# Four small layers on one core: factor sums shared with POOL, the last batch in query halves, due times by kind

## The chip, the cores and the metric

One core of one Trainium2 chip runs the whole program; the time is device microseconds of one execution, with everything read from and written to the chip's main memory inside it. A core has engines that run side by side, each with its own queue in a fixed order: PE (TensorE: matmuls, and transposes, which are matmuls with an identity), DVE (VectorE), ACT (ScalarE) and POOL (GpSimd). SP (SyncE) only issues transfers here; POOL issues some too. They wait for each other through semaphores. The times are medians of a few executions; the profile is of one further execution of the same kernel.

## The reference

All inputs are float32. The input x has 8 batches of 512 tokens by 512 features, and four layers follow, each with a layer norm before and another before its residual add:

```
x = x + LN(attn0(LN(x)))     # scores = x^T x over the token axis, softmax, context
x = x + LN(ffn0(LN(x)))      # sum over r of x @ factors[r], r = 0..7, / sqrt(8) + bias
x = x + LN(attn1(LN(x)))     # RMS norm, 8 query heads of 64, 2 key/value heads, Wo, skip
x = x + LN(ffn1(LN(x)))      # silu(x Wg * gs) * (x Wu * us), then Wd * ds; inner width 1408
```

Since the eight factor matrices meet the same x, their sum is made once, and one product with it serves. Gate, up and down weights are -1, 0 or 1.

## The kernel before

**Tiles.** A token tile is 128 tokens, so a batch has four (NT = 4), and the 512 features make four k tiles (KT = 4). The inner width of the last layer makes eleven inner tiles (NI = 11), kept in two tensors, hd0 with inner tiles 0 to 5 and hd1 with 6 to 10. Only one of each exists. The other tags used below: x (11 tiles), z and hl (2 each), e and wgu (4 each), and in PSUM five banks f and three banks g. Most matmuls are in full float32. The last layer's x and hd are split into a leading and a remaining part of a cheaper format, since its weights are exact in that format.

**Order.** Nothing is written down in the order in which it runs. Each stage records operations with an engine, an estimated duration, what they read and write, and a due time (`rec.prio`), counted in batches. `Recorder.issue` (L108) then plays the whole program with those estimates, and at each step, on each engine, takes among the operations that could start within `slack` of the first one that with the least due time; a buffer is taken when its first user starts and comes free after its last. The order so found is the order of each engine's queue on the chip, where it doesn't change any more. On PE an operation has a `state`, the shape in which it uses the array: 128x128, 64x128 (scores and transposes of attention 1, two row groups at once) or 128x64 (its weighted values, two column groups). A change of state costs 0.1 us in that reckoning. Stages of neighbouring batches overlap: while the second attention of batch b runs, the last layer of batch b-1 fills PE.

**The start.** `load_fixed` (L388) reads eight factor matrices in four k tiles each. For each k tile the first factor goes straight to `fsum` and the other seven to places of hd0 and hd1, from which DVE adds them in turn (L401), 28 adds in all. `look_at_low_bits` (L420) reads all gate, up and down weights once more into hd0 and hd1 and ORs them on DVE (33 operations, L442), into a z tile, to learn whether the cheaper format is exact; a second version of the program runs only if it is not. Weight loads of the last layer are issued by POOL (L372), the others by SP (L351).

**The stages.** `stage_attn0` makes scores row by row (L626, with transposes for the lower part, L624), a softmax (L551 maximum, L558 exponential, L568, L575), its transpose, and the context (L655). `stage_ffn0` takes a norm (L495 statistics, L500, L504 and L511 on POOL for the inverse deviation, L519 the normalize), transposes the tile (L587), multiplies by `fsum` (L677) and adds (L690). `add_layernorm` norms the result and adds it to x on POOL (L537). `stage_attn1` makes keys, values and queries (L809, L820, L838), for each of four head pairs and each query tile the scores (L869), softmax, transposes (L900), copies (L912), and for each two query tiles the weighted values (L931); then it projects the four token tiles (L959, L974). Its loops run over head pairs outside and halves of the query tiles inside. `stage_ffn1` norms and transposes the four token tiles, splits them (L990, L999), multiplies by gate and up (L1032, over 512 tokens), makes hd (L1052, L1062, L1071), splits it again, multiplies by down (L1100), scales (L1113), norms, adds and stores (L1123).

Of the kernel before, what the change touches and what calls it, by code (L numbers as in the profile page):

```python
# [12 lines left out]
I32 = mybir.dt.int32  # L13
# [40 lines left out]
class Recorder:  # L54
# [53 lines left out]
    def issue(self, places, slack=0.1):  # L108
# [26 lines left out]
        while left:  # L135
            best = None
            for e, ops in ready.items():
                able = [(s, op.prio, op.n, op) for op in ops if (s := start(op)) is not None]
                if not able:
                    continue  # L140
                first = min(able)[0]
                pick = min((p, n, s, op) for s, p, n, op in able if s <= first + slack)
                if best is None or (pick[2], pick[1]) < best[:2]:
                    best = (pick[2], pick[1], pick[3])
# [93 lines left out]
def layers(  # L238
# [99 lines left out]


# [48 lines left out]
    def load_fixed():  # L388
        rec.prio = 0.15

        slots = staging()
        for kt in range(KT):
            rec.prio = 0.15 + 0.01 * kt
            load(fsum, factors[0, ts(kt, P), :], part=kt, view=lambda t, kt=kt: t[:, kt, :])
            for r in range(1, R):
                f, j = next(slots)
                load(f, factors[r, ts(kt, P), :], part=j, view=lambda t, j=j: t[:, j, :])

                def go(f=f, j=j, kt=kt):
                    d = fsum.t[:, kt, :]  # L400
                    nc.vector.tensor_tensor(d, d, f.t[:, j, :], ALU.add)  # L401

                add("DVE", 0.69, go, reads=[(f, j)], writes=[(fsum, kt)])
        load(bias_bc, ffn_bias.partition_broadcast(P))
        rec.prio = 0.3
# [7 lines left out]
        rec.prio = 0.95  # L413
# [6 lines left out]
    def look_at_low_bits():  # L420

        low, most, total = Buf("z"), Buf("s1"), Buf("f")
        rec.prio = 1.0
        bits = lambda: low.t[:, :].bitcast(I32)
        add("DVE", 0.3, lambda: nc.vector.memset(bits(), 0), writes=[low])
        slots = staging()
        pieces = [(w, c) for w in (gate_t, up_t, down_t) for c in range(NI)]
        for n, (w, c) in enumerate(pieces):
            rec.prio = 1.0 + 0.01 * n
            raw, j = next(slots)  # L430
            if w is down_t:
                load(raw, w[ts(c, P), :], part=j, view=lambda t, j=j: t[:, j, :])
            else:
                load(
                    raw,
                    w[:, ts(c, P)].rearrange("(k p) n -> p k n", p=P),
                    part=j,
                    view=lambda t, j=j: blocks(t[:, j, :]),
                )

            def gather(raw=raw, j=j):
                nc.vector.tensor_tensor(  # L442
                    bits(), bits(), raw.t[:, j, :].bitcast(I32), ALU.bitwise_or
                )

            add("DVE", 0.69, gather, reads=[(raw, j)], writes=[low])
# [83 lines left out]
    def add_layernorm(xt, src, us=0.55):  # L530

        y = buf_of(src) if buf_of(src).tag == "z" else Buf("z")
        layernorm(whole(y), src, us)
        add(
            "POOL",
            1.27,
            lambda: nc.gpsimd.tensor_tensor(ap(xt), ap(xt), y.t[:, :], ALU.add),  # L537
# [69 lines left out]
    def stage_attn0(x, at, span):  # L607
        xn, xnT, wT = Buf("big"), Buf("big"), Buf("big")
        rec.prio = at
# [7 lines left out]
        for i in range(KT):  # L617
            rec.prio = at + span * (0.1 + 0.1 * i)
# [30 lines left out]
        for t in range(NT):  # L649
            rec.prio = at + span * (0.5 + 0.1 * t)  # L650
# [15 lines left out]
    def stage_ffn0(x, at, span):  # L666
        for t in range(NT):
            rec.prio = at + span * 0.2 * t
# [29 lines left out]
    def stage_attn1(x, at, span):  # L698
# [3 lines left out]
        for t in range(NT):  # L702
            rec.prio = at + span * 0.05 * t
# [97 lines left out]
        rec.prio = at + span * 0.2  # L801
# [28 lines left out]

        for i in range(NPAIR):
            rec.prio = at + span * (0.22 + 0.13 * i)
# [13 lines left out]
            asked = mm(pq, 3.43, queries, [wq, hT], room=[qT])  # L846
# [10 lines left out]
        wos = []  # L857
        for i in range(NPAIR):
            for u in range(2):
                aT = Buf("big")  # L860
                for s in (2 * u, 2 * u + 1):
                    rec.prio = at + span * (0.25 + 0.13 * i + 0.03 * s)
                    es = [Buf("e") for _ in range(G)]
                    scs = [Buf("f") for _ in range(G)]

                    def scores(i=i, s=s, scs=scs):
                        for g in range(G):
                            gp = ts(g, DH)
                            nc.tensor.matmul(  # L869
                                scs[g].t[:, :],  # L870
                                qT.t[gp, i, ts(s, P)],
                                kT.t[gp, :],
                                start=True,
                                stop=True,
                            )

                    add(
                        "PE",
                        0.87,
                        scores,  # L880
                        reads=[(qT, (i, u)), kT],
                        writes=scs,
                        room=[*es, aT],
                        state="64x128",
                    )
                    for g in range(G):
                        softmax_row(scs[g], es[g])


                    pts = [Buf("f") for _ in range(2)]  # L890

                    def halves(b):
                        return b.t[:, :].rearrange("p (c q) -> p c q", q=DH)

                    def transposes(es=es, pts=pts):
                        for g in range(G):
                            for t in range(NT):
                                for hf in range(2):
                                    hp = ts(hf, DH)
                                    nc.tensor.transpose(  # L900
                                        halves(pts[hf])[:, g * NT + t, :],
                                        es[g].t[hp, ts(t, P)],
                                        ident[hp, hp],
                                    )

                    add("PE", 0.56, transposes, reads=es, writes=pts, room=[aT], state="64x128")
                    for hf in range(2):

                        def place(hf=hf, s=s, aT=aT, pts=pts):
                            lo = s % 2 * P + hf * DH  # L910
                            copy = nc.scalar.copy
                            copy(columns_of(aT)[:, :, lo : lo + DH], halves(pts[hf]))  # L912

                        add(
                            "ACT",
                            0.6,
                            place,
                            reads=[pts[hf]],
                            writes=[(aT, 2 * s + hf)],
                        )  # L920
                rec.prio = at + span * (0.29 + 0.13 * i + 0.03 * s)
                po = Buf("f")

                def columns_of(b):
                    return flat(b.t).rearrange("p (c q) -> p c q", q=2 * P)

                def values_of(aT=aT, po=po):
                    for t in range(NT):
                        for g in range(G):
                            gp = ts(g, DH)  # L930
                            nc.tensor.matmul(  # L931
                                po.t[gp, : 2 * P],
                                v.t[:, t * P + g * DH : t * P + (g + 1) * DH],
                                columns_of(aT)[:, g * NT + t, :],
                                start=(t == 0),
                                stop=(t == NT - 1),
                            )

                attended = mm(po, 1.75, values_of, [aT, v], state="128x64")

                add(
                    "ACT",
                    0.4,
                    lambda i=i, u=u, po=po: nc.scalar.copy(
                        qT.t[:, i, ts(u, 2 * P)], po.t[:, : 2 * P]
                    ),
                    reads=[po],
                    writes=[(qT, (i, u))],
                )
            wos.append(Buf("ws"))  # L950
            load(wos[i], wo_t[ts(i, P), :], view=flat, after=[asked])

        for t in range(NT):
            rec.prio = at + span * (0.8 + 0.03 * t)
# [25 lines left out]
            add_layernorm(whole(x[t]), whole(z))  # L980
        return last
# [24 lines left out]
    def stage_ffn1(x, b, at, span, after):  # L1006
        PASS = 0.23 if split else 0.86
        xs = [Buf("hl") for _ in range(1 + split)]
        for t in range(NT):
            rec.prio = at + span * 0.01 * t  # L1010
            xn = Buf("row")
            mv, rstd = moments(whole(x[t]))
            normalize(whole(xn), whole(x[t]), mv, rstd, room=xs)
            pt = transpose_to(column(xs[0], t), whole(xn), copy=None, room=xs)
            in_parts([column(d, t) for d in xs], lambda pt=pt: blocks(pt.t), [pt], 0.6)

        hds = [Buf(f"hd{c}") for c in range(len(CUTS))]
        for c, (lo, hi) in enumerate(CUTS):
# [182 lines left out]
```

## Time and profile before

| what | value |
|---|---|
| median of 3 runs (lowest, highest) | 1568.37 us (1568.25, 1568.81) |
| the profiled execution | 1568.29 us |
| its span, first to last instruction | 1566.5 us |
| PE, DVE, ACT, POOL busy | 1503.5, 1080.4, 702.2, 566.4 us |
| mean clock of PE | 0.988 of full |
| moved by DMA | 105.87 MB, mean 68 GB/s |
| PE busy in 600:700 and in 700:800 | 100.00 and 98.10 us |

How to read the lines that follow. A line of the timeline gives start and length in microseconds, the engine, the line of the kernel, the operation, what it writes and reads, the shape, how many instructions are merged (x8), and in brackets how long the engine stood idle before it and what ended that. Matmuls overlap, so their lengths are a little longer than the distance from one to the next. A line of waits gives the total, how often and the longest. A full float32 product counts as two instructions. "Clock" is the share of PE's full clock that was granted.

### The profile page before, as it was taken

Reading aid. Unit: us, or ns where it says so; the run is one execution under the profiler, and the core shown is the slowest. Engines: PE = TensorE matmul, PEld = TensorE weight load, DVE = VectorE, ACT = ScalarE, POOL = GpSimd, SP = SyncE. Lnnn points to the kernel's source line nnn. Section 1 sums busy time; section 2 is a strip of 40 time slices with the busy share of each in tenths; the row PEclk is TensorE's granted clock in tenths of the full one; section 3 lists DMA queues with packets and bytes.
Section 4 is the critical chain, followed back from the end, with each engine's and each line's share of the span. In section 5 each row is a group of like instructions: output and inputs, shape, how many; then the busy total and the mean of one; then the engine's idle time right before and its main releaser. Section 6 shows DMA issues by size and latency. Waiting matters only on the chain.

```text
span 1566.5 us, 21966 instructions
## 1 busy us (share of the span) xinstructions
PE 1503.5 (96%) x7986; PEld 923.6 (59%) x7986; DVE 1080.4 (69%) x2226; ACT 702.2 (45%) x1448; POOL 566.4 (36%) x869
## 2 busy tenths in 40 slices
PE   6799999999999999999999999999999999999896
PEld 3354456665666646665566656666566665666485
DVE  6898865679557794587845788458865678557734
ACT  2045546541376324763257523575236742277221
POOL 3614341137410473115721257103651036411532
PEclk9899999999999999999999999999999999999999
DMA  9540043212331124302142132411233102330170
GB/s 346 165 155 1 1 101 75 44 52 54 74 75 28 41 57 91 62 28 72 30 89 53 40 75 42 88 35 48 61 61 81 21 34 61 74 75 14 35 132 31
DMA packets 152471, 105.87 MB, mean 68 GB/s; under 512 B 6945, under 2 KB 132897, under 8 KB 152353
## 3 DMA queue, kind: packets, MB, share of 16 engines
q0 software_dynamic: 94512, 49.03, 16.5%
q1 hardware_dynamic: 57840, 55.34, 11.3%
q8 instruction: 65, 1.06, 0.3%
q14 instruction: 54, 0.43, 0.1%
HBM read 95.96 MB, written 8.39 MB: 67 GB/s over the span
## 4 chain that ended last, share of the span: by engine, by line
PE 81%; DVE 9%; POOL 5%; DMA 2%; issue 2%; ACT 1%; SPq 0%; POOLq 0%; ACTq 0%; DVEq 0%
PE g L1032 21%; PE g L1100 11%; PE f L869 8%; PE f L931 7%; PE f L838 7%; PE f L677 7%; PE f L900 5%; PE f L959 4%; PE f L587 3%; PE f L626 3%; DVE row L519 3%; POOL rstd L511 2%; DVE st L495 2%; PE f L820 2%; PE f L809 2%
## 5 line engine op out<-in xcount | busy, mean ns | idle before, releaser
L1032 PE MATMUL g<-hl,wgu 128*128 128x512 f32 x1408 | 350.3, 400 | 0.7 <-ACT hl L990 0.7
L551 DVE TENSOR_REDUCE s<-f 128x1 f32<-128x512 f32 x288 | 186.5, 683 | 185.3 <-PE f L869 171.3
L1032 PEld LDWEIGHTS g<-hl,wgu 128*128 128x128 f32 x1408 | 258.9, 189 | 81.5 <-issue 18.4
L504 POOL TENSOR_SCALAR ve<-mv 128x1 f32<-128x1 f32 x224 | 71.1, 317 | 523.0 <-DVE mv L500 509.0
L558 ACT ACTIVATE e<-f,s 128x512 f32<-128x512 f32 x288 | 195.8, 688 | 87.0 <-DVE s L551 81.2
L537 POOL TENSOR_TENSOR x<-x,z 128x512 f32<-128x512 f32 x128 | 169.5, 1324 | 61.6 <-DVE z L519 53.1
L1100 PE MATMUL g<-wd,hl 128*128 128x512 f32 x704 | 180.7, 406 | 3.2 <-DVE hl L999 3.2
L912 ACT COPY big<-f 128x512 f32<-128x512 f32 x256 | 134.4, 597 | 60.1 <-PE f L900 59.2
L1100 PEld LDWEIGHTS g<-wd,hl 128*128 128x128 f32 x704 | 129.0, 189 | 45.0 <-issue 11.5
L372 POOL DMA_DIRECT2D wgu<-in_up_t x88 | 67.3, 765 | 235.9 <-PE g L1032 235.8
L575 DVE TENSOR_SCALAR e<-e,s 128x512 f32<-128x512 f32 x288 | 144.0, 500 | 10.2
L511 POOL TENSOR_TENSOR rstd<-ve,mhalf 128x1 f32<-128x1 f32 x224 | 143.1, 639 | 18.1
L869 PE MATMUL f<-kv,big 64*128 64x512 f32 x512 | 138.6, 628 | 0.0
L1062 DVE SCALAR_TENSOR_TENSOR sig<-g,gs,sig 128x512 f32<-128x512 f32 x88 | 65.8, 748 | 98.4 <-ACT sig L1052 98.4
L931 PE MATMUL f<-big,kv 128*64 128x256 f32 x1024 | 124.6, 385 | 0.0
L372 POOL DMA_DIRECT2D wgu<-in_gate_t x88 | 68.7, 781 | 140.3 <-PE g L1032 137.1
L677 PE MATMUL f<-fsum,rT 128*128 128x512 f32 x256 | 116.7, 604 | 0.7 <-ACT rT L591 0.7
L959 PE MATMUL f<-ws,big 128*128 128x512 f32 x256 | 114.9, 594 | 0.6 <-ACT big L794 0.6
L838 PE MATMUL f<-big,ws 128*128 128x512 f32 x256 | 114.1, 594 | 0.0
L655 PE MATMUL f<-big,big 128*128 128x512 f32 x256 | 112.3, 594 | 0.7 <-ACT big L591 0.7
L931 PEld LDWEIGHTS f<-big,kv 128*64 128x64 f32 x1024 | 67.8, 136 | 71.8 <-ACT big L912 13.8
L900 PEld LDWEIGHTS f<-ident,e 64*128 64x128 f32 x2048 | 71.7, 139 | 43.7 <-issue 32.0
(81 smaller groups left out, 1971.3 us busy)
## 6 DMA issues: line engine op xcount, KB each, us to landing
wgu<-in_gate_t POOLq DMA_DIRECT2D x88, 256.0 KB, 3.3
wgu<-in_up_t POOLq DMA_DIRECT2D x88, 256.0 KB, 3.4
x<-in_x SPq DMA_DIRECT2D x32, 256.0 KB, 2.7
ws<-in_wq_t SPq DMA_DIRECT2D x32, 256.0 KB, 3.3
ws<-in_wo_t SPq DMA_DIRECT2D x32, 256.0 KB, 2.6
out<-x SPq DMA_DIRECT2D x32, 256.0 KB, 2.0
hd<-in_factors SPq DMA_DIRECT2D x28, 256.0 KB, 5.4
wd<-in_down_t POOLq DMA_DIRECT2D x11, 256.0 KB, 8.1
```

Source lines behind the costliest of these rows:

```text
L511: lambda: nc.gpsimd.tensor_tensor(rstd.t[:, :], ve.t[:, :], mhalf, ALU.pow),
L537: lambda: nc.gpsimd.tensor_tensor(ap(xt), ap(xt), y.t[:, :], ALU.add),
L551: lambda: nc.vector.tensor_reduce(nmax.t[:, :], sc.t[:, :], AX.X, ALU.max, negate=True),
L558: lambda: nc.scalar.activation(e.t[:, :], sc.t[:, :], AF.Exp, bias=nmax.t[:, :], accum_out=tot.t[:, :]),
L677: nc.tensor.matmul(po.t[:, :], xnT.t[:, kt, :], fsum.t[:, kt, :], start=(kt == 0), stop=(kt == KT - 1),)
L838: nc.tensor.matmul(pq.t[:, :], wq.t[:, kt, :], hT.t[:, kt, :], start=(kt == 0), stop=(kt == KT - 1),)
L869: nc.tensor.matmul(scs[g].t[:, :], qT.t[gp, i, ts(s, P)], kT.t[gp, :], start=True, stop=True,)
L900: nc.tensor.transpose(halves(pts[hf])[:, g * NT + t, :], es[g].t[hp, ts(t, P)], ident[hp, hp],)
L931: nc.tensor.matmul(po.t[gp, : 2 * P], v.t[:, t * P + g * DH : t * P + (g + 1) * DH], columns_of(aT)[:, g * NT + t, :], start=(t == 0), sto ...
L959: nc.tensor.matmul(po.t[:, :], qT.t[:, i, ts(t, P)], flat(wos[i].t), start=(i == 0), stop=(i == NPAIR - 1),)
L1032: nc.tensor.matmul(bank.t[:, :], w.t[:, kt, :], d.t[:, kt, :], start=(n == 0), stop=(n == KT * len(xs) - 1),)
L1100: nc.tensor.matmul(po.t[:, :], ap(o)[:, it - lo, :], wd.t[:, it, :], start=(it == 0 and k == 0), stop=(it == NI - 1 and k == len(ops) - 1),)
```

## The change

- **Factor sums.** For k tiles 0 and 3 (`FSUM_POOL`) the seven adds each are made by POOL; tiles 1 and 2 stay on DVE.
- **Low bits.** The running OR moves from a z tile to a piece of hd, cleared by POOL, and gets later due times.
- **Last batch, second attention** (`EARLY`): the loops are turned, so that both query tiles of a half go through all head pairs and are projected before the second half begins. Wo is loaded with the first half.
- **Last batch, last layer:** norms by halves of the tokens, then the gate and up products of inner tiles 0 to 3 (`FEW`) for tokens 0 to 255 and, loaded again, for tokens 256 to 511; the other seven for all tokens. Down products are recorded after all of these.
- **Residual adds of the last batch** in attention 1 and the last layer go from POOL to DVE.
- **Order.** Due times come from a table, by kind of work and batch (`DUE`, `SHIFT`), slack is 0.1198, and on PE an operation in another state than the one held has 0.0066 added to its due time (`STAY`). Steps in the table count head pairs, halves, tiles. The gate step of the last batch is negative.

```diff
+                held = state.get(e)
+                pick = min(
+                    (p + (STAY.get(e, 0.0) if op.state not in (None, held) else 0.0), n, s, op)
+                    for s, p, n, op in able
+                    if s <= first + slack
+                )
...
+    def when(kind, b, *steps):
+        rec.prio = due(kind, b if b < B // 2 else b - B, B, *steps)
...
+                eng, us, on = (
+                    ("POOL", 1.27, nc.gpsimd) if kt in FSUM_POOL else ("DVE", 0.69, nc.vector)
+                )
...
-        low, most, total = Buf("z"), Buf("s1"), Buf("f")
+        most, total = Buf("s1"), Buf("f")
+        slots = staging()
+        low = next(slots)
+        add("POOL", 0.5, lambda: nc.gpsimd.memset(bits(), 0), writes=[low])
...
+        eng, took, on = ("DVE", 0.69, nc.vector) if last else ("POOL", 1.27, nc.gpsimd)
...
+        if split_up:
+            for u in range(2):
+                for i in range(NPAIR):
+                    attended = attend(i, u)
+                    if u == 0:
+                        load_wo(i)
+                for t in (2 * u, 2 * u + 1):
+                    when(kinds[2], b, t % 2, u)
+                    last = project(t, attended)
+                firsts.append(last)
...
+        if b in EARLY or b - B in EARLY:
+            rounds = [((0, 1), range(FEW)), ((2, 3), range(FEW)), (every, range(FEW, NI))]
+            kind = "h1."
...
+                    sig = Buf("sig" if len(toks) == NT else "e")
+                    pg, pu = Buf("g"), Buf("g" if len(toks) == NT else "f")
...
+                                        bank.t[:, cut],
+                                        w.t[:, kt, :],
+                                        d.t[:, kt, cut],
...
+                    after=products,
...
-AHEAD = 0.3
-ATTN0 = (0.0, 0.163)
-FFN0 = (0.476, 0.16)
-ATTN1 = (0.55, 0.6)
-FFN1 = (1.682, 0.337)
+DUE = {
+    "x": (0.0595,),
+    "fsum": (0.0844, 0.01),
+    "wd": (1.1173,),
+    "low": (1.3155, 0.01),
+    "a0.norm": (0.0803,),
+    "a0.row": (0.0175, 0.0195),
+    "a0.out": (0.2134, 0.0139),
+    "f0": (0.3719, 0.0331),
+    "a1.norm": (0.6166, 0.0452),
+    "a1.q": (0.6808, 0.1115),
+    "a1.row": (0.6967, 0.0723, 0.036, 0.0208),
+    "a1.mix": (0.7469, 0.0737, 0.036),
+    "a1.out": (1.0283, 0.0236),
+    "e1.row": (0.6591, 0.039, 0.1695, 0.0034),
+    "e1.mix": (0.9942, 0.0607, 0.1848),
+    "e1.out": (0.9884, 0.018, 0.141),
+    "f1.norm": (1.7342, 0.0089),
+    "f1.gate": (1.716, 0.0146),
+    "f1.down": (1.935, 0.019, 0.0131),
+    "h1.norm": (1.7316, -0.021, 0.095),
+    "h1.gate": (1.1851, -0.0129, 0.0932),
+    "h1.down": (1.935, 0.0236, 0.0091),
...
+SHIFT = {
+    ("a0", 0): -0.112,
+    ("a1", 0): 0.183,
+    ("f1", 0): -0.0585,
+    ("x", 1): 0.0585,
...
+STAY = {"PE": 0.0066}
+SLACK = 0.1198
+FSUM_POOL = (0, 3)
+EARLY = (-1,)
+FEW = 4
...
+def due(kind, b, n, *steps):
+    first, *more = DUE[kind]
+    at = first + (b if b >= 0 else b + n) + SHIFT.get((kind[:2], b), 0.0)
+    return at + sum(k * d for k, d in zip(steps, more))
```

## The prediction

> **What bounds the kernel now.** I read the page first, then PE's busy time by stretches, then the list of what PE waited for, then the timeline at the start, in a middle batch and at the end. The first fence is the page's busy line and two of PE's waits (total us, times, longest).
>
> ```profile
> PE 1503.5 (96%) x7986; PEld 923.6 (59%) x7986; DVE 1080.4 (69%) x2226; ACT 702.2 (45%) x1448; POOL 566.4 (36%) x869
> ...
> PE f L587 <- DVE row L519: 27.2, 12, 8.5
> PE f L624 <- ACT u L640: 3.7, 2, 3.1
> ```
>
> PE is the bound: 1503.5 of 1566.5 us, so all of its idle time is 63 us. Only two things can be won: that idle time, and work on PE that isn't arithmetic. The stretches tell where the idle time lies (columns: start and end, length, busy us of PE, PEld, DVE, ACT, POOL, then PE's clock).
>
> ```profile
> 0.00:57.26 57.26, 34.33 (x114) 19.93 (x115) 42.68 (x82) 10.96 (x22) 26.68 (x51) 0.91 0.95 308
> 57.26:61.50 4.24, 4.24 (x7) 1.86 (x7) 2.91 (x7) 0.59 (x1) 2.57 (x7) 0.57 0.22 62
> 1477.80:1488.80 11.00, 4.02 (x17) 2.58 (x17) 8.67 (x17) 2.39 (x5) 9.33 (x15) 0.64 0.32 59
> 1488.80:1493.00 4.20, 4.20 (x9) 3.08 (x10) 0.66 (x1) 1.33 (x2) 0.00 (x0) 0.50 0.51 94
> ```
>
> Before the first product with the factor sum, 57.26 us, PE idles for 23 us, and then runs four more at little over half clock. Ahead of the last batch's gate products PE does almost nothing for 11 us, and then starts cold. A stretch of 100 us in the middle shows PE at 98.1 to 100.0, and the waits there are one of 1.8 us per batch. After PE's last product at 1554.05 come 12.4 us of norm, add and store.
>
> **The start.** DVE holds it: 8.9 of every 10 us from 20 to 60. In its queue the 28 factor adds (20.1 us, 721 ns each in the group row) stand between the softmax rows and norms that PE waits for.
>
> ```profile
> 16.54 0.69 DVE L401 TENSOR_TENSOR fsum<-fsum,hd 128x512 f32<-128x512 f32 x1 [4.20 <-DMA hd<-in_factors]
> 23.09 0.33 PE L624 MATMUL f<-ident,u 128*128 128x128 f32 x1 [3.14 <-ACT u L640]
> 44.47 1.26 POOL L537 TENSOR_TENSOR x<-x,z 128x512 f32<-128x512 f32 x1 [0.93 <-DVE z L519]
> 45.12 1.88 DVE L401 TENSOR_TENSOR fsum<-fsum,hd 128x512 f32<-128x512 f32 x2
> 55.35 2.12 PE L587 MATMUL f<-ident,row 128*128 128x128 f32 x8 [8.46 <-DVE row L519]
> ```
>
> The first line shows DVE standing for a factor that hasn't landed, with batch 0's row maxima queued behind it; 3.14 of PE's wait follow from that. The last shows PE waiting 8.46 for the norm of the first tile of the factor layer, whose x was done at 41.84, but whose statistics stand in DVE's queue until 52.52, after the last add.
>
> What the change does here: k tiles 0 and 3 go to POOL, 14 adds. DVE loses 14 x 0.721 = 10.1 us, and the first landings, with 5.6 us of DVE waits in all, are waited for on POOL (0.00 busy from 20 to 30), where no norm of batch 0 stands behind them until 37. POOL gains 14 x 1.26 = 17.6 us by the L537 line above (1.65 where it was held up at 40.19). Tile 3's seven, about 9 us, fall where POOL also has the four norms and adds of the first layer, 2.05 each uncontended, so 17 us of POOL work from about 31 on. The eleven wd issues in POOL's queue are through by 13.2, before the first landing at 16.5, so the adds wait for none of them. What is queued behind a POOL add that waits for a late factor is the rstd of those norms; DVE's normalize waits for it, then PE. Batch 1's four x loads are due after the factors now, so the factor loads stand earlier in SP's queue: eight x loads take 4.72 us there before the first factor at 5.50, four of them about 2.4. The 33 loads and 33 ORs of the low bit check (757 ns each, 25 us of DVE, now in 52 to 136) move behind batch 1's first layers, and their running OR leaves the z tile for a piece of hd, so one of two z tiles comes free for the norms until 136 (counted at nothing: DVE sets the pace there). They hide under a DVE that is 57% busy from 200 to 300; without that cover they delay batch 0's gate products, since both use the hd tiles.
>
> Here a rule of the Trainium skill speaks against the change ("SBUF — State Buffer", Who interferes with whom): a DVE instruction with two SBUF inputs and a POOL instruction that reads SBUF exclude each other for the whole instruction. The trace agrees: the two adds at 45.12 take 1.88 and not 1.38, the extra 0.50 being about the rest of POOL's add from 44.47. By the group rows alone, DVE is relieved of 10.1 and up to 5.6 of waits: up to 15.7 earlier, limited by PE's contexts, which end at 46.9 and would end some 3 earlier. By the rule the adds hold the shared port 14 x 0.69 + 14 x 1.26 = 27.3 us in place of 19.3, so 8.0 of it come back: 2 to 8 earlier. Tile 0's adds fall where DVE has little that needs the port, so I charge the lock for tile 3's: 7 x (1.26 - 0.69) = 4.0. With half of the waits recovered, 10.1 + 2.0 - 4.0 makes 8. **Start: -8**, bounds -12 and 0.
>
> **The last batch.** Its second attention runs query tiles 0 and 1 through all four head pairs, projects them, then tiles 2 and 3. The gate and up products of inner tiles 0 to 3 are made once for each half of the tokens.
>
> ```profile
> 1467.22 10.57 PE L959 MATMUL f<-ws,big 128*128 128x512 f32 x24
> ...
> 1488.79 42.99 PE L1032 MATMUL g<-hl,wgu 128*128 128x512 f32 x176 [0.68 <-ACT hl L990]
> ...
> 1533.49 20.56 PE L1100 MATMUL g<-wd,hl 128*128 128x512 f32 x87 [1.36 <-DVE hl L999]
> ...
> 1557.34 1.26 POOL L537 TENSOR_TENSOR x<-x,z 128x512 f32<-128x512 f32 x1 [0.66 <-DVE z L519]
> ```
>
> From the end of the projections at 1477.79 to the first gate product is 11.0 us, a chain of two norms that nothing covers. The first half's products are 4 x 2 x 8 = 64 matmuls over 256 columns, which no row shows. Two bounds: half of the 512 column price (16 take 3.75 in a middle batch, 234 ns each), 117 ns; or the pace of weight loads, if these can't keep up, 189 ns by the mean of their row. Near is L820, where 32 loads and matmuls of 128 f32 columns go at 112 ns each, so a load can hide at that pace. I take 117: 64 x 0.117 = 7.5 us of cover, and no cost against 512 columns (at 189 ns the 128 half products would cost 128 x 0.072 = 9 us more). PE can use these products as filler under attention too; the sum is the same, since PE is full up to 1477.8.
>
> Cold clock: 176 products at 234 ns are 41.25, so 42.99 holds 1.7 of it. The skill ("TensorE: Matmul & The Clock Gate", What's actually happening) puts the clock down to half after an idle window of about 3.4 us. Two gaps of 2.5 with short transposes between them were enough here (0.64, then 0.50). After the change about 3.5 us of the 11 stay bare: by the rule on the edge, and the 1.7 would come back; by the row, it takes more idling than that. I count them won.
>
> The last batch's residual adds go to DVE: 0.69 in place of 1.26, 0.57 off the final chain; the same 0.57 in the covered chain count for nothing. Against it: inner tiles 10 down to 4 now come in falling order, so the first half of hd is finished last. The down products' first cast then waits for the last product's eviction, where now only hl is waited for (PE's 1.36 above): +1.0 by the 0.75 of L1071 and a hop. Eight weight slices are loaded twice, 8 x 0.77 = 6.2 us of issue on POOL, each ahead of an rstd in POOL's queue; 0.84 to 0.94 of such delay is in the chain already, and the first half's products cover it. **End: -7.5 - 1.7 - 0.6 + 1.0 = -9**, bounds -12 and 0.
>
> **The middle.** Two things can move.
>
> ```profile
> 626.50 1.13 PE L869 MATMUL f<-kv,big 64*128 64x512 f32 x4
> 627.56 1.95 PE L931 MATMUL f<-big,kv 128*64 128x256 f32 x16
> ...
> 756.08 1.58 DVE L519 TENSOR_SCALAR row<-x,mv,rstd 128x512 f32<-128x512 f32 x1
> ...
> 757.72 0.66 PE L587 MATMUL f<-ident,row 128*128 128x128 f32 x4 [1.84 <-DVE row L519]
> ```
>
> The gap first: PE stands 1.84 us, since its queue has the second tile's transposes ahead of the first tile's product, and the normalize took 1.58 and not 0.55 beside a POOL add. New due times may reorder this in six batches, 0 to -11; there is nothing in them aimed at that place, so I take four tenths, -4.5. Then the array's shape: 8 scores take 1.92 from start to start, 4 take 1.06, so a change of shape (64*128, 128*64, 128*128) costs 1.06 - 0.86 = 0.2. From 588 to 776 I count 46 changes in PE's timeline, some 9 us per batch. STAY adds 0.0066 to the due time of work in another shape, against 0.0146 between gate tiles: a nudge. Five f banks force most changes. I take two fewer per batch, 2 x 0.2 x 7 = -2.8; bounds -9 and +6. **Middle: -7.**
>
> **Sum:** 1568.3 (this execution, 1.8 around its span) - 8 - 9 - 7 = 1544; it stands within 0.1 of the median of the runs, so that holds for both.
>
> **Rivals.** Chances in brackets.
> - The forecast, 1540 to 1548 and what is near (0.38).
> - The port lock eats the start (0.17): POOL, with 17 us of norms and adds from 31 on, holds up the factor layer as DVE did. For it: 1.58 for a normalize, 0.66 for a 0.22 row. Against: tile 0's adds lie apart. Start -2: 1550.
> - The due times do nothing in the middle (0.17): gap and shape changes stay. For it: gates still start at 0.716 and downs at 0.935 of a batch. 1551.
> - The middle gains fully (0.16), gap closed and six changes fewer: -11 - 8: 1532. For it: PE's shapes follow due times where both are ready. Against: five banks.
> - Slower (0.08): the gate products run ahead of the attention rows that they fill in. An unfilled pair of rows has a chain of 0.68 + 0.89 + 0.16 + 0.49 and again 0.68 on DVE and ACT against 1.35 on PE: some 1.5 of idling. With 17 won at the edges, two of 16 pairs unfilled in seven batches (21 us) decide; at four (42), 1593. Against: the gates' span of 0.146 (0.169 now) shrinks by little against the rows'.
> - The same (0.04): one such pair, 10 us, and edges that win half: 1568.
>
> The range takes the forecast with both 155x cases and the edge of the gaining one: 1529 to 1562. Under 0.2% (3 us), no change could be told from this kernel's runs. Faster 0.88, same 0.04, slower 0.08.
>
> **What would show it.** Right: first product with fsum near 49 and DVE's waits for factors gone; after the last projection, PE's gap under 4 us; last add on DVE, 0.69; 40 to 45 shape changes a batch; the L1032 row over 256 columns near 117 ns. Wrong, if L537 and the factor adds on POOL take 1.6 and more while PE waits as long at f0; if PE's middle falls below 98 of 100; if half products run at 189.

## The result and the profile after

The changed kernel takes 1547.93 us (median of 4 runs, 1546.74 to 1550.57), the kernel before beside it 1568.31; the ratio is 0.9873 (0.9856 to 0.9891), 20.4 us. The forecast was 1544, with a range of 1529 to 1562. The page's busy line of after and its longest waits on PE (total us, times, longest):

```profile
PE 1499.7 (97%) x8050; PEld 927.7 (60%) x8050; DVE 1078.3 (70%) x2227; ACT 688.6 (45%) x1440; POOL 576.2 (37%) x884
...
PE f L603 <- DVE row L534: 12.8, 12, 3.4
PE f L603 <- DVE big L534: 7.8, 1, 7.8
...
PE g L1094 <- DMA wgu<-in_gate_t: 3.3, 4, 1.3
PE g L1162 <- ACT hl L1035: 1.7, 1, 1.7
```

Lines have moved: transposes L587 are L603 now, factor adds L401 are L413, scores L626 are L642, products with fsum L677 are L693, projections L959 are L972, gate and up L1032 are L1094, down L1100 is L1162. PE's idle time fell by 16.3 us (63.0 to 46.7) and its busy time by 3.8. The wait for the normalize of a row, 27.2 before, is halved, and two kinds of wait are new: for a weight slice, and for the first split of hd.

To see where, I cut both executions at the same events: the first scores of batches 1, 2 and 7 (the first 128x512 scores of a batch). Windows of PE (start and end, length, busy us), before and then after:

```profile
0.00:75.12 75.12, 52.19 (x167) 28.85 (x168) 57.05 (x108) 13.35 (x27) 36.07 (x66) 0.91 0.82 261
75.12:336.21 261.09, 254.40 (x1507) 149.33 (x1506) 194.55 (x428) 138.37 (x307) 76.47 (x120) 0.99 0.25 63
336.21:1277.88 941.67, 931.43 (x5024) 572.44 (x5022) 653.91 (x1352) 445.39 (x912) 345.00 (x529) 1.00 0.25 56
```

```profile
0.00:65.61 65.61, 47.68 (x155) 25.57 (x156) 45.61 (x86) 13.00 (x26) 48.89 (x78) 0.95 0.90 281
65.61:324.97 259.36, 254.59 (x1510) 150.04 (x1509) 204.98 (x433) 136.93 (x302) 81.35 (x125) 0.99 0.28 69
324.97:1257.84 932.87, 928.04 (x5001) 572.69 (x4999) 645.51 (x1350) 432.71 (x901) 343.99 (x528) 1.00 0.25 57
```

Batch 2 begins 11.2 us earlier, the five batches after it take 8.8 less, and from the first scores of the last batch to the end it is 288.6 us in both. So the end seems to have won nothing. That reading is wrong by itself: a cut at an event also moves when other work moves past it. Behind the last cut 98 more matmuls stand than before (1394 and 1296); 64 of them come from the half products, which count twice, and most of the others are weighted values and transposes that had stood ahead of the cut. Idle time is safer: 29.6 to 22.7 up to batch 2, 10.2 to 4.8 in the five batches, 23.1 to 19.2 in the rest.

The start of after, first two adds that meet (POOL and DVE), then POOL's queue later on, then PE, from the timeline:

```profile
18.89 1.82 POOL L413 TENSOR_TENSOR fsum<-fsum,hd 128x512 f32<-128x512 f32 x1
...
19.61 1.64 DVE L413 TENSOR_TENSOR fsum<-fsum,hd 128x512 f32<-128x512 f32 x1
```

```profile
39.63 5.30 POOL L413 TENSOR_TENSOR fsum<-fsum,hd 128x512 f32<-128x512 f32 x4
44.90 0.23 POOL L519 TENSOR_SCALAR ve<-mv 128x1 f32<-128x1 f32 x1
```

```profile
30.15 15.43 PE L671 MATMUL f<-big,big 128*128 128x512 f32 x32 [0.67 <-ACT big L607]
49.03 0.66 PE L603 MATMUL f<-ident,row 128*128 128x128 f32 x4 [3.45 <-DVE row L534]
50.45 5.21 PE L693 MATMUL f<-fsum,rT 128*128 128x512 f32 x8 [0.77 <-ACT rT L607]
```

The first product with the factor sum starts at 50.45 and not 57.26; PE's bare stretch ahead of it shrinks from 8.46 to 3.45. The lock shows where two adds meet, and only there: at 18.9 us POOL's takes 1.82 and not 1.26, DVE's next one 1.64 and not 0.69, and it happens once more at 32.5 to 35.7 us. The other 11 of POOL's 14 adds take 1.26 to 1.34. The second fence shows a new wait that the forecast only named: by 41.0 us the statistics of two norms are done, but POOL's queue begins their inverse deviations (rstd) only at 44.90, behind four adds. The end of after:

```profile
1458.38 3.60 PE L972 MATMUL f<-ws,big 128*128 128x512 f32 x8
1462.77 1.12 PE L1094 MATMUL f<-hl,wgu 128*128 128x256 f32 x8
...
1466.82 1.19 PE L1094 MATMUL g<-hl,wgu 128*128 128x256 f32 x8 [1.01 <-DMA wgu<-in_gate_t]
...
1470.47 0.66 PE L603 MATMUL f<-ident,row 128*128 128x128 f32 x4 [1.32 <-DVE row L534]
...
1473.12 0.39 PE L1094 MATMUL g<-hl,wgu 128*128 128x256 f32 x1 [0.67 <-ACT hl L1035]
1473.85 1.86 PE L1094 MATMUL g<-hl,wgu 128*128 128x256 f32 x7 [0.34 <-DVE hl L1044]
...
1513.18 0.49 PE L1162 MATMUL g<-wd,hl 128*128 128x512 f32 x1 [1.71 <-ACT hl L1035]
1514.17 22.39 PE L1162 MATMUL g<-wd,hl 128*128 128x512 f32 x87 [0.50 <-DVE hl L1044]
```

The half products do stand in the gap, at 120 ns each (eight start at 1462.77, the next eight at 1463.73). Yet from the last projection's end at 1461.98 to the second half's first product at 1473.12 it is 11.1 us, as long as before (11.0): 48 half products fill 5.8 us of it, and 3.7 stay bare. And the 87 down products take 22.39, where 20.56 had been enough.

### The profile page after: what moved, and what is told of

Read it like the earlier page. It is cut to its first block, busy times and chain, and to the rows that moved or that the text cites. A ratio compares the mean times of both kernels' runs of the same rounds, so it can differ in the third digit from the quotient of the medians.

```text
span 1546.4 us, 22104 instructions
## 1 busy us (share of the span) xinstructions
PE 1499.7 (97%) x8050; PEld 927.7 (60%) x8050; DVE 1078.3 (70%) x2227; ACT 688.6 (45%) x1440; POOL 576.2 (37%) x884
## 3 DMA queue, kind: packets, MB, share of 16 engines
q0 software_dynamic: 98736, 51.13, 17.5%
## 4 chain that ended last, share of the span: by engine, by line
PE 74%; POOL 11%; DVE 10%; issue 2%; DMA 2%; ACT 0%; SPq 0%; POOLq 0%; DVEq 0%
PE g L1094 16%; PE g L1162 11%; PE f L884 8%; PE f L946 8%; PE f L855 7%; PE f L972 5%; PE f L915 5%; POOL rstd L526 3%; PE f L642 3%; POOL x L553 3%; PE f L671 3%; DVE row L534 2%; PE f L603 2%; DVE st L510 2%; PE f L836 2%
## 5 line engine op out<-in xcount | busy, mean ns | idle before, releaser
L1094 PE MATMUL g<-hl,wgu 128*128 128x512 f32 (+1 forms) x1408 | 343.2, 395 | 5.5 <-DMA wgu<-in_gate_t 3.3
L1094 PEld LDWEIGHTS g<-hl,wgu 128*128 128x128 f32 x1408 | 254.7, 189 | 80.8 <-issue 12.5
L1162 PE MATMUL g<-wd,hl 128*128 128x512 f32 x704 | 180.6, 407 | 2.2 <-ACT hl L1035 1.7
L553 POOL TENSOR_TENSOR x<-x,z 128x512 f32<-128x512 f32 x120 | 158.1, 1318 | 59.5 <-DVE z L534 38.1
L591 DVE TENSOR_SCALAR e<-e,s 128x512 f32<-128x512 f32 x288 | 152.3, 529 | 10.2
L1162 PEld LDWEIGHTS g<-wd,hl 128*128 128x128 f32 x704 | 129.3, 190 | 48.0 <-issue 16.0
L381 POOL DMA_DIRECT2D wgu<-in_gate_t x92 | 73.4, 798 | 167.1 <-PE g L1094 161.8
L884 PE MATMUL f<-kv,big 64*128 64x512 f32 x512 | 132.9, 619 | 0.0
L381 POOL DMA_DIRECT2D wgu<-in_up_t x92 | 70.6, 768 | 129.6 <-PE g L1094 127.7
L693 PE MATMUL f<-fsum,rT 128*128 128x512 f32 x256 | 116.7, 603 | 1.3 <-ACT rT L607 1.2
L855 PE MATMUL f<-big,ws 128*128 128x512 f32 x256 | 118.0, 605 | 0.0
L972 PE MATMUL f<-ws,big 128*128 128x512 f32 x256 | 115.8, 596 | 0.0
```

The costliest lines, as they stand in the source:

```text
L553: lambda: on.tensor_tensor(ap(xt), ap(xt), y.t[:, :], ALU.add),
L591: lambda: nc.vector.tensor_scalar(e.t[:, :], e.t[:, :], rtot.t[:, :], None, ALU.mult),
L855: nc.tensor.matmul(pq.t[:, :], wq.t[:, kt, :], hT.t[:, kt, :], start=(kt == 0), stop=(kt == KT - 1),)
L884: nc.tensor.matmul(scs[g].t[:, :], qT.t[gp, i, ts(s, P)], kT.t[gp, :], start=True, stop=True,)
L972: nc.tensor.matmul(po.t[:, :], qT.t[:, i, ts(t, P)], flat(wos[i].t), start=(i == 0), stop=(i == NPAIR - 1),)
L1094: nc.tensor.matmul(bank.t[:, cut], w.t[:, kt, :], d.t[:, kt, cut], start=(n == 0), stop=(n == KT * len(xs) - 1),)
```

## Experiments

Medians are against the kernel before on the same chip (1568.1 to 1568.4), and "tail" is the time from the first scores of the last batch to PE's last product in the profile, which a late first load can't blur: 276.2 before, 278.7 after. It compares kernels with the same due times; between others, work moves past its cut. For these I count work: all matmuls that PE has started by a fixed time, each at the pace of its shape at full clock (429 ns for a float32 product over 512 columns, 227 to 235 for one of the last layer, 120 for a half product, 109 for a transpose of 128x128, those of the second attention by the mean of a run). This is an estimate from the traces; the last three kernels have the same due times and parts up to 1250 us, and lie within 1.4 us of each other. Lead over the kernel before, in us of PE's work, and the lead at PE's last product:

| kernel | by 325 | by 1250 | last product |
|---|---|---|---|
| b_pool (sums) | 6.4 | 6.1 | 6.7 |
| due_only (due times) | -4.2 | 1.5 | -0.4 |
| x_sums_dve (due times, halves) | -3.3 | 2.3 | 4.2 |
| o_parts (sums, halves) | -0.9 | -1.1 | -0.9 |
| x_no_halves (due times, sums) | 10.0 | 14.9 | 13.5 |
| x_few0 (all but half products) | 9.1 | 14.4 | 17.4 |
| after | 10.5 | 15.3 | 17.5 |

**x_sums_dve: all factor adds back on DVE**

```diff
-FSUM_POOL = (0, 3)
+FSUM_POOL = ()
```

> The changed kernel with all 28 factor adds back on DVE; due times, halves and the rest stay. If the adds on POOL make the start (11.2 us earlier at the first scores of batch 2), this loses 7 to 12 us: 1555 to 1560. If the new due times make the start and the port lock eats what POOL takes over, it loses less than 3: 1548 to 1551.

1562.09 us, 14.2 slower than the changed kernel, more than either theory. Batch 2's first scores come at 340.6, later than before the change (336.2), and batch 1's at 104.1 and not 65.6. The new due times without POOL's help make a worse start than the old ones.

**b_pool: the kernel before with that part alone**

```diff
+                eng, us, on = (
+                    ("POOL", 1.27, nc.gpsimd) if kt in (0, 3) else ("DVE", 0.69, nc.vector)
+                )
...
-                    nc.vector.tensor_tensor(d, d, f.t[:, j, :], ALU.add)
-
-                add("DVE", 0.69, go, reads=[(f, j)], writes=[(fsum, kt)])
+                    on.tensor_tensor(d, d, f.t[:, j, :], ALU.add)
+
+                add(eng, us, go, reads=[(f, j)], writes=[(fsum, kt)])
```

> The kernel before with one edit: k tiles 0 and 3 of the factor sums on POOL. By the forecast's step 8 us faster: 1560. If the lock on the shared port eats it, at most 2: 1566. If adds on POOL only pay together with due times that give DVE's freed time to batch 0, about 1564.

1561.97 us, ratio 0.9965 (0.9951 to 0.9979), 6.4 faster; batch 2's scores come 6.6 earlier and everything after runs as before (periods of 187.6). In the first 325 us PE is busy for 303.2 us here, 302.3 in the changed kernel, 295.4 before; but time at half clock counts as busy too, and of matmuls 1637 have begun here, 1663 there, 1586 before. So the sums alone give 6.4 of the 10.5 that the start gains, and the rest comes from the new due times beside them, which alone lose 4.2 there (due_only).

**x_no_halves: the last batch like the others**

```diff
-EARLY = (-1,)
+EARLY = ()
```

> The changed kernel with the last batch treated like the others (second attention by head pairs, all inner tiles over all tokens); its residual adds stay on DVE. By the forecast's step the halves are worth 8 us: 1556. By the trace of after, in which the stretch from the first scores of the last batch to the end is as long as before (288.6 us in both), they are worth 0 to 2: 1548 to 1550. If the eight extra weight loads and the cold clock cost more than the cover gives, it is faster: 1545.

1555.21 us, 7.3 slower; the tail is 282.4. Up to the last batch it runs as the changed kernel does (first scores at 1258.2 and 1257.8). The reading from the cut alone had said 0 to 2 and falls. This tail is 6.2 longer than before the change, mostly because work has moved past the cut: by the count of work the lead falls by 1.4 from 1250 us to the last product. On this chip b_pool took 1561.97, so one way from the kernel before to the changed one is 6.4 for the sums, then 6.8 for the due times with all that is small (0.6 of it the adds on DVE), then 7.3 for the halves.

**x_few0: halves in the second attention, no half products**

```diff
-FEW = 4
+FEW = 0
```

> The changed kernel with the second attention of the last batch by halves, but no inner tile taken for half of the tokens (FEW 0). If the half products are the cover, the gain of the halves (7.3) is lost: 1555. If the earlier projection and norms of the first half give it, most stays: 1549. If the eight extra loads and the second chain cost as much as the cover gives, it is the faster one: 1546.

1549.64 us (1547.85 to 1550.93), which overlaps the runs of the changed kernel. PE at its end, beside x_no_halves in the second fence:

```profile
1454.03 7.03 PE L972 MATMUL f<-ws,big 128*128 128x512 f32 x16
...
1469.93 41.84 PE L1094 MATMUL g<-hl,wgu 128*128 128x512 f32 x176 [0.68 <-ACT hl L1035]
```

```profile
1450.47 10.57 PE L972 MATMUL f<-ws,big 128*128 128x512 f32 x24
...
1475.06 42.97 PE L1094 MATMUL g<-hl,wgu 128*128 128x512 f32 x176 [0.68 <-ACT hl L1035]
```

With bare halves and nothing to cover it the gap is 8.9 us (1461.06 to 1469.93); without halves 14.0 (1461.04 to 1475.06), on the old due times 11.0. Two norms instead of four stand in DVE's and POOL's queues after the last projection. The tail is 277.7, 1.0 shorter than with the half products. So on PE the gain of the halves is the earlier projection and norm of two tiles, and the half products add nothing to it. By the medians x_few0 keeps 5.6 of the 7.3; the other 1.7 is no more than the runs scatter, and about what the end of the program, behind PE, takes longer here (last section).

**no_reload: the second half's early products without their own loads**

```diff
+                    if q == 1:
+                        wg = wu = wd
+                    else:
...
+                            wt = blocks(w.t[:, it, :]) if w is wd else w.t
...
-                                        w.t[:, kt, :],
+                                        wt[:, kt, :],
```

> The changed kernel, but the half products of tokens 256 to 511 take their weights from resident down weights and not from a second load: eight loads fewer, a wrong result for those products, the same work on PE. If the second loads cost PE its DMA waits (3.3) and hold up the norms in POOL's queue (some 2), it gains 3 to 5: 1544. If these waits lie inside a chain that is as long anyway, under 1: 1547.5.

The products of inner tiles 0 to 3 for tokens 256 to 511 use the down weights here. 1547.73 us, no difference in the medians. The profile is of an execution of 1553.2 us, which is 5.2 us behind that of the changed kernel already at the first scores of the last batch; the tail leaves that out. PE's waits for gate slices after 1440 fall from 2.9 to 1.0 and the tail from 278.7 to 276.7, so the second loads cost PE 2 us; why the median doesn't show it follows under what was unexpected.

**up and few0_up: inner tiles in rising order**

```diff
-    "h1.gate": (1.1851, -0.0129, 0.0932),
+    "h1.gate": (1.0561, 0.0129, 0.0932),
```

few0_up has FEW = 0 besides.

> The changed kernel with the last batch's inner tiles in rising order, the half products kept. By the same theory 2.4 faster than the changed kernel: 1545.5. If the order doesn't matter: 1548. If rising order breaks the way in which half and whole products alternate, slower: 1550.

> FEW 0 as in x_few0, and the last batch's inner tiles in rising order, so that the first half of hd is complete early. If the wait ahead of the down products (1.71 + 0.49) and the cold clock behind it (87 products in 22.2 us, 20.6 when warm) come from the falling order, it gains 2.4 on x_few0: 1547.2, and the wait goes back to 1.4. If they come from the hl tiles alone, as in the kernel before, no gain: 1549.6.

1546.48 (1545.48 to 1547.43) and 1547.37. The tails are 276.8 and 276.0, 1.9 and 1.7 shorter than with falling order. PE in up:

```profile
1514.96 20.86 PE L1162 MATMUL g<-wd,hl 128*128 128x512 f32 x87 [1.36 <-DVE hl L1044]
```

The wait is back at 1.36 where it was 1.71 and 0.50, and the down products run at full clock: 20.86 and not 22.39. The wait goes with the order: it is 1.36 in all kernels without the falling order and 1.71 and 0.5 in all seven with it. The cold clock (half clock) behind it doesn't always follow: in two of the seven, x_sums_dve and stay_half, the products stay at full clock after the same waits. PE in x_sums_dve:

```profile
1529.01 20.85 PE L1162 MATMUL g<-wd,hl 128*128 128x512 f32 x87 [0.49 <-DVE hl L1044]
```

So the falling order costs 0.85 us each time, and 1.5 more in some executions. The medians of up and the changed kernel lie 1.5 apart, up being the fastest kernel of all; their intervals overlap (0.9842 to 0.9875 against 0.9856 to 0.9891), so the better tail is read from the profile and not proved by the runs.

**due_only: neither part**

```diff
-FSUM_POOL = (0, 3)
+FSUM_POOL = ()
-EARLY = (-1,)
+EARLY = ()
```

> The changed kernel without both large parts: all factor adds on DVE and the last batch like the others. What stays is the table of due times, STAY and the last batch's adds on DVE. If the parts add up, 1548 + 14 + 7 = 1569, no gain over before: the table earns nothing alone. By the forecast's middle step it keeps 7: 1561. If the table only fits the kernel with its parts, it is slower than before: 1575.

1567.48 us, ratio 0.9997 (0.9988 to 1.0006): nothing. The five middle batches take 10.6 us less (931.1), the start 5.1 more (341.4) and the tail 5.8 more (282.0), part of which is work moved past the cuts; by the count of work it is 4.2 behind at 325 us and 1.5 ahead at 1250. The table gains nothing alone; beside the sums it gains 6.8 (x_no_halves against b_pool).

**o_parts: both parts on the old due times**

```diff
-    "a0.out": (0.2134, 0.0139),
+    "a0.out": (0.0815, 0.0163),
...
-    "f0": (0.3719, 0.0331),
+    "f0": (0.476, 0.032),
...
-STAY = {"PE": 0.0066}
+STAY = {}
```

> The changed kernel with the due times of before written as a table (the last batch's halves keep theirs), slack 0.1 and no STAY: both parts on the old due times. If the parts carry the gain, 6 for the sums and 7 for the halves: 1555. If they need the new due times, 1561 or more. If the old due times without STAY break as the new ones do without it, above 1580.

1567.15 us: nothing either. The tail is 276.1, as before, so the halves give nothing where the old due times already end well. Batch 2 begins at 337.1, 7.5 later than in b_pool; PE waits for softmax rows there and idles 12.4 us in batch 1 and not 6.3. So the 6.4 that the sums gave in b_pool are lost here. This kernel also keeps the running OR in hd and has the last adds on DVE; which of it undoes the sums I didn't separate.

**x_no_stay, stay_half and b_stay: the 0.0066**

```diff
-STAY = {"PE": 0.0066}
+STAY = {}
```

> The changed kernel without the 0.0066 for work in another shape of the array. If it is what brought the changes of shape from 243 to 225 in the five middle batches, they go back to about 243 and it loses 4 to 5 us in all: 1552. If the due times did that, it loses under 1.

> The changed kernel with STAY halved to 0.0033. If the value acts smoothly between none (1604) and 0.0066 (1548), about 1575. If it only has to be there, 1548 to 1552. If the order reacts to any such step by chance, anything from 1548 to 1604, with other waits than without STAY.

> The kernel before with one edit: 0.0066 on the due time of PE work in another shape. The forecast gives two changes of shape fewer per batch, -3: 1565. If STAY is a main gain in itself, -10: 1558. If it only serves the new table (without it that table took 1604), within 2 of before, either way.

1603.78 without it, 1605.21 with half of it, and 1569.70 when the kernel before gets it (ratio 1.0010, 1.0004 to 1.0017). In the kernel before it takes the changes of shape from 378 to 355 and gains nothing: PE's busy time falls by 1.5 us only, and its idle time grows by 3.8. In the changed kernel, leaving it out costs 56 us: PE idles 80 us and not 47, and is busy 23 longer, at 0.97 of its clock in the stretches with gaps (500 to 600 and 700 to 800 us). PE of x_no_stay in the middle:

```profile
787.98 0.66 PE L603 MATMUL f<-ident,row 128*128 128x128 f32 x4 [2.69 <-DVE row L534]
792.36 1.11 PE L603 MATMUL f<-ident,row 128*128 128x128 f32 x4 [3.73 <-DVE s L765]
```

The last head pair's rows there run from 715 to 742, after the next batch's scores have begun at 711.8; the projections end at 755, and two norm chains follow with nothing to fill PE. Periods are 172 to 210 us where 186 to 188 were had. The loss comes whole somewhere between 0.0066 and 0.0033 and not by degrees: these due times work with the order that 0.0066 gives.

## Why the prediction was right, step by step, and where not

The time fell inside the range, 3.9 us above the forecast. By the count of work the start gave 10.5 (forecast 8), the middle 4.8 (7) and the end 4.8 (9; 2.2 of it up to PE's last product, 0.6 the adds on DVE, 2.0 the end of the program behind the last add, of the last section). So that the sum came near is in part luck: the start gained more than its step said, and the end less and not by the term named.

- **Start, -8: right in its path, and more in size.** b_pool gives 6.4 by the runs and 6.6 by batch 2; the new due times make 10.5 of it. The first product of the factor layer comes at 50.45 (forecast 49). DVE's waits for factors fall from 5.6 to 2.3 us and are not gone. The lock is there, but only three POOL adds and two of DVE's meet it, 3.1 us in all, where 4.0 was charged for seven meetings. The rival in which the lock eats the start falls, though its path is there: the inverse deviations that wait behind four POOL adds. In the sum, half of 5.6 is 2.8 and not 2.0. Not seen ahead: the contexts run partly cold (15.43 and not 14.00).
- **Middle, -7: the gap right, the changes of shape not.** Between the cuts the five batches take 8.8 less: idle time 10.2 to 4.8 (-5.4, forecast -4.5 for six batches) and busy time -3.4. But of this 3.4 some 2.3 is work that now stands behind the cut (16 weighted values, eight transposes). So 18 fewer changes (243 to 225) are left with 1 us, where the 0.2 of the forecast would make 3.6. In b_stay 23 fewer go with 1.5 us of busy time, in x_no_halves beside b_pool 21 fewer with 4.0; the price of a change stays open. The product of the factor layer now follows two transposes closely; the gap of 1.84 is 0.23:

```profile
742.20 3.67 PE L693 MATMUL f<-fsum,rT 128*128 128x512 f32 x8
...
752.25 0.66 PE L603 MATMUL f<-ident,row 128*128 128x128 f32 x4 [0.23 <-DVE row L534]
```

  What the forecast missed is that the table's gain depends on the parts: nothing alone (due_only), 6.8 beside the sums.
- **End, -9: the step that failed.** The halves are worth 7.3 on the new due times (x_no_halves), near the number by luck, and nothing on the old ones (o_parts). "64 x 0.117 = 7.5 us of cover" is what the sum rested on. They cover, and PE's bare 3.7 us are close to the 3.5 forecast; but the sum took the chain as fixed and its loads as covered. Without cover the halves alone shorten the chain from 14.0 to 8.9 (x_few0); with it the chain is 11.1, and behind it PE waits 1.9 for weight slices, which no_reload doesn't. In POOL's queue the inverse deviation of the last tile stands behind two weight loads; in DVE's the statistics of x stand among hd products:

```profile
1468.38 0.82 POOL L381 DMA_DIRECT2D wgu<-in_gate_t  x1
1469.45 0.74 POOL L381 DMA_DIRECT2D wgu<-in_up_t  x1 [0.25 <-PE f L1094]
1470.21 0.28 POOL L519 TENSOR_SCALAR ve<-mv 128x1 f32<-128x1 f32 x1
```

  The statistics were done at 1468.4; the norm's first step runs at 1470.21. The sum had priced these issues (6.2 us) and then called them covered by the very products whose weights they load. x_few0, with no cover at all, has the shorter tail. What gives most of the 7.3 is that half of the projection and norm work leaves the end of the chain, which the sum counted at nothing.
- **Cold clock, -1.7: wrong.** With 3.7 us of bare waits in the gap the clock still fell, and the second half's first products run cold (seven in 1.66 us, where eight take 0.96 warm). In this execution the wait of 1.71 + 0.50 ahead of the down products makes these cold too, 1.5 us (22.39 against 20.86 in up).
- **Falling order, +1.0: right**, 0.85 by the wait (2.21 against 1.36), with the cold clock that can follow it not in the sum.
- **Adds on DVE, -0.6: right.** From PE's last product to the last add it is 4.55 before, 3.94 after.
- **Half product, 117 ns:** 120 measured. **Shape changes** 40 to 45 a batch: 44 to 46, from 48.6 (243 in five batches; the 46 counted ahead were a little few).
- The rival that the due times do nothing holds for them alone (due_only), and fails in the company of the sums. The slower rival is what happens without STAY: rows that come late and norm chains that nothing fills. It was given 0.08 because gate and row dues move together; what decided was not there but in a constant that the sum valued at 2.8 us.

## What to carry to other kernels

Taking work off the engine whose queue holds up the first layer paid by itself here (b_pool), and can be tried alone; o_parts shows that another edit can lose it again. Work put in a gap as cover must not send its own loads and evictions through the queues in which the gap's chain runs; shortening the chain (two tiles instead of four behind it) gave the gain on PE, and cover on top of it none. In a program whose order comes from due times, the constants fit each other: the table alone and the parts on the old order are worth nothing, STAY alone loses 1.4 us, together they win 20, and one of them removed costs up to 56. So taking one part out tells what the rest depends on and not what the part is worth. And a cut at an event of the program compares two orders only if the work behind the cut is the same.

## What was not expected of the hardware

From the last add to the end of the span it takes 5.8 to 6.0 us in the six kernels that load weight slices a second time (after, up, x_sums_dve, o_parts, x_no_stay, stay_half) and 7.3 to 7.9 in the other eight. The last store doesn't decide it: from issue to landing it takes 2.0 to 3.3 us, and about 3.0 in both up and few0_up, which end 5.9 and 7.6 after their last add. In the traces the eight have a pause of 1.3 to 2.1 us between two of SyncE's closing semaphore instructions, which the six don't have. That hides the 1.0 us which the half products cost, and the 2 us won by no_reload, and it is about 2 of the 20.4 us in all; I have no cause for it.

PE's clock fell to half after a wait of 1.71 and one of 0.50 us with a single product between (0.81 over 1509 to 1518), and held after one of 1.36 (1.00 over 1511 to 1516 in up). But the length of the waits doesn't decide it alone: after the same 1.71 and 0.49 it held in x_sums_dve (1.00 over 1524 to 1533) and in stay_half (1.00 over 1568 to 1577). What else decides is open.
